# Ternary product in three bfloat16 parts, and one run for the keys and values of the latent attention

## The chip, the core and the metric

The kernel runs on one core of a Trainium2 chip. The metric is the device time of one execution in microseconds (us). TensorE is called PE here (its weight loads PEld), VectorE DVE, ScalarE ACT, GpSimd POOL, and SyncE SP; SP issues the transfers.

## The reference, cut to what matters

The input is 128 batches of 32 rows of 256 numbers (`x`) and 128 contexts of 257 rows of 256 (`ctx`). Six residual stages follow each other, each on rows normalised to mean 0 and variance 1. Stages 3 and 5 are the ones that the change touches:

```python
x = x + xattn0(ctx, layernorm(x))            # softmax attention of the rows on the context
x = x + selective_scan(layernorm(x))         # 512 channels, 16 states, a recurrence over 32 steps
x = x + ternary_ffn(layernorm(x))            # 256 -> 1024 -> 256
x = x + linear_attention(layernorm(x), ctx)
x = x + latent_attention(layernorm(x))       # 16 heads, latent of 64
x = x + quantised_ffn(layernorm(x))          # 8-bit rows, ternary weights

# ternary_ffn
h = layernorm(x) @ ternary(W_fc).T           # ternary: every weight is -1, 0 or 1
h = gelu(h); h = layernorm(h) * ln_w + ln_b
y = h @ ternary(W_proj).T

# latent_attention
lat = (x @ W_k + x @ W_v) @ W_down           # 64 numbers for a row
k = lat @ W_up_k; v = lat @ W_up_v; q = x @ W_q
s = (q . k) / 16 * exp(-0.01 * |i - j|); out = softmax(s) @ v; y = out @ W_o
```

## The kernel before, in words

The 4096 rows are 32 groups of 128 rows (four batches each), one row in each partition. `BLOCKS = (2, 4, 4, 4, 4, 4, 4, 4, 2)` puts the groups in nine blocks. For each group, `context_group` loads the context, forms keys and values (tiles `pkey`, `ku`, `pval`, `vf`, `pk`) and does the first attention. For each block, `scan_block` does the recurrence: four channel chunks of 16 states, and for every state an exponential on ACT (tile `a`), a scan on DVE (tile `h`) and a multiply-add on DVE (tile `acc`), 64 of each in a block; `pproj` holds the projections that go in, `pout` the product that comes out. Then `latent_group` runs four steps for each group: `mlp` (the ternary feed-forward), `linear`, `attention` (the latent attention) and `quantized_mlp`.

Nothing of this is issued in the order in which it is written. `Recorder.record` (L312) collects every operation with the engines that could do it and an assumed duration (`ns_of`, L42); `Recorder.order` (L378) then plays the whole program through in a list schedule: at each step it takes, among the operations that can start soon, the one that is due first. The due times come from the table `DUE` (L1445), one pair of start and end for each numbered part of the program (`begin`, L306, opens a part); `PRICE`, `WINDOW`, `SOONER`, `AHEAD` and `HORIZON` (L554) weigh the choice of an engine, how far a later start is allowed for an earlier due time, how early transfers are asked for, and how far ahead a tile may be opened. `R.either` is an operation for DVE or POOL, `R.copy` one for ACT or DVE. `together` (L276) joins a run of PE instructions into one step. `Recorder.trace` (L537) issues the result; L540 is the line that issues nearly everything, so the profile shows L540 for nearly all instructions and the tile names tell them apart. Each engine issues its list in that fixed order.

The PSUM tiles come from a ring of eight banks, the SBUF tiles from rings of 4 KB (`t4k`), 2 KB (`t2k`, 15 of them) and 1 KB (`t1k`, 7).

In `mlp` (L1171) the rows are transposed unnormalised and uncentred (`rows_T`, tile `xT`); the weights `w_fc` are float32 and have had the mean over the 256 inputs taken off in the set-up (`centred(w_fc, 2)`, L897), so that the product needs no centred rows. For each half of the 1024 outputs, two float32 matmuls fill a bank (tile `ph`):

```python
for k in range(2):
    ph = bank("ph")
    cols = slice(k * 512, (k + 1) * 512)
    with R.together():
        accumulate(ph, [(xT[:, dc, :], w_fc[:, dc, cols]) for dc in range(2)])
```

In `attention` (L1247) the queries (bank `pqa`, tile `qTa`), the latent (bank `plat`, tile `lat`), the keys (bank `pka`, tile `kd`), the scores (banks `psa`) and the softmax (tile `ea`) come one after the other; the values (bank `pva`, tile `vd`) are computed behind the softmax. ACT copies `qTa` ahead of `lat`.

Of the kernel before, what the change touches and what calls it, by code (L numbers as in the profile page):

```python
# [16 lines left out]
P = 128  # L17
# [74 lines left out]
    return 450  # L92


TAIL = {"vector": 75, "scalar": 100, "gpsimd": 25, "tensor": 130, "sync": 0}
HOP = {"vector": 38, "scalar": 38, "gpsimd": 80, "tensor": 55, "sync": 100}
TABLES = {AF.Exp: "exp", AF.Gelu: "gelu", AF.Sigmoid: "sigmoid"}
TABLE_NS = 1300
# [10 lines left out]
def size_of(a):  # L109
    n = 1  # L110
    for k in a.shape[1:]:
        n *= k
    return n
# [153 lines left out]
class Recorder:  # L267
# [8 lines left out]
    def together(self):  # L276

        recorder = self

        class Joined:  # L280
            def __enter__(self):
                recorder.joined = []

            def __exit__(self, *_):
                parts, recorder.joined = recorder.joined, None
                ways = {"tensor": ([c for p in parts for c in p[0]], sum(p[1] for p in parts), False)}
                recorder.add(ways, [r for p in parts for r in p[2]], [w for p in parts for w in p[3]])

        return Joined()

    def copy(self, out, in_):
        self.record({"scalar": ("copy", (out, in_), {}), "vector": ("tensor_copy", (out, in_), {})})

    def relu(self, out, in_):
        self.record({
# [10 lines left out]
    def begin(self, stage):  # L306

        self.stage = stage
        self.group += 1
        self.spans[self.group] = DUE[self.group]  # L310

    def record(self, calls):  # L312
# [31 lines left out]
        self.keep += bufs  # L344
        self.bufs_of.update((id(b), b) for b in bufs)
        if self.joined is not None:
            self.joined.append((*ways["tensor"][:2], reads, writes))
            return
        landing = 0
        if "sync" in ways:  # L350
# [200 lines left out]
                last[op.engine] = ins  # L551


PRICE = {"tensor": 0.0, "vector": 3.195, "scalar": 3.454, "gpsimd": 8.58, "sync": 0.0}  # L554
WINDOW = 31.919
SOONER = -0.015
AHEAD = 0
HORIZON = 0.832


@with_exitstack
def perceiver_kernel(ctx: ExitStack, tc: tile.TileContext, t: dict, out: bass.AP):
# [90 lines left out]
        return ring("t4", 4).tile(shape, name)  # L653

    def t2k(shape, name, dtype=F32):
        return ring("t2", 15).tile(shape, name, dtype)

    def t1k(shape, name, dtype=F32):
        return ring("t1", 7).tile(shape, name, dtype)
# [45 lines left out]
    R.begin("s")  # L705
    wqk = wts.tile([P, 2, D], F32, name="wqk")
    wkd = wts.tile([P, 2, LAT], F32, name="wkd")
    w_fc = wts.tile([P, 2, HID], F32, name="w_fc")
    w_pr = wts.tile([P, 8, D], F32, name="w_pr")
    s0 = wts.tile([P, D], F32, name="s0")  # L710
    w1 = wts.tile([P, 2, HID], BF16, name="w1")
# [132 lines left out]
    def late_setup():  # L844
# [49 lines left out]
                )  # L894

        ternary(w_fc, rows(t["w_fcT"]), [P, 2, HID], "fc", 1e-6, False)
        centred(w_fc, 2)  # L897
        ternary(w_pr, rows(t["w_prT"]), [P, 8, D], "pr", 1e-6, False)
        ternary(w1, rows(t["w1T"]), [P, 2, HID], "w1", 1e-5, True, g1)
        ternary(w2, rows(t["w2T"]), [P, 8, D], "w2", 1e-5, True, g2)  # L900
# [53 lines left out]
    def context_group(b0, xg, kvc):  # L954
# [83 lines left out]
            accumulate(py[:, 0:D], [(oT[:, dc, :], wv0[:, dc, :]) for dc in range(2)])  # L1038
        R.vector.scalar_tensor_tensor(xg, py[:, 0:D], rs, xg, ALU.mult, ALU.add)

        pk4 = bank("pk")
# [71 lines left out]
    def scan_block(x):  # L1115
# [15 lines left out]
        for ic in range(4):  # L1131
            pg = project(w_gate, ic * P)
            yg.append(t2k([P, TOK], "yg")[:, 0:tok])
            R.scalar.activation(yg[ic], pg, AF.Sigmoid, bias=b_gate[:, ic : ic + 1])
        for ic in range(4):

            dl = t2k([P, TOK], "dl")[:, 0:tok]
            R.scalar.activation(
                dl, project(w_in, DI + ic * P), AF.Relu, bias=b_in[:, 4 + ic : 5 + ic]
            )  # L1140
            xd = project(w_in, ic * P)
            acc = bank("acc")[:, 0:tok]
            R.scalar.activation(
                acc, xd, AF.Identity, bias=bd_in[:, ic : ic + 1], scale=d_vec[:, ic : ic + 1]
            )
            R.vector.scalar_tensor_tensor(xd, xd, b_in[:, ic : ic + 1], dl, ALU.add, ALU.mult)
            dv = dl.rearrange("p (b q) -> p b q", q=LQ)
            for s in range(NST):

                a = a_ring[s % NA][:, 0:batches, :]  # L1150
                R.scalar.activation(
                    a[:, :, 1:LQ], dv[:, :, 1:LQ], AF.Exp, scale=a_neg[:, ic, s : s + 1]
                )
                h = t2k([P, TOK], "h")[:, 0:tok]
                R.vector.tensor_tensor_scan(
                    h, a.rearrange("p b q -> p (b q)"), xd, 0.0, ALU.mult, ALU.add
                )
                R.vector.scalar_tensor_tensor(
                    acc, h, w_st[:, ic, s : s + 1], acc, ALU.mult, ALU.add
                )  # L1160
            R.vector.tensor_tensor(yg[ic], acc, yg[ic], ALU.mult)
        for g in range(size):
            po = bank("pout")
            with R.together():
                accumulate(
                    po[:, 0:D], [(yg[ic][:, g * P : (g + 1) * P], w_out[:, ic, :]) for ic in range(4)]
                )
            R.vector.tensor_tensor(x[g], po[:, 0:D], x[g], ALU.add)


    def mlp(xg):  # L1171

        _, r = stats(xg)
        xT = rows_T(xg)
        R.gpsimd.tensor_tensor(xg, xg, s0, ALU.add)
        hid = t4k([P, HID], "hid")
        st = tiny("st2", [P, 2, 6])
        for k in range(2):
            ph = bank("ph")
            cols = slice(k * 512, (k + 1) * 512)  # L1180
            with R.together():
                accumulate(ph, [(xT[:, dc, :], w_fc[:, dc, cols]) for dc in range(2)])
            R.scalar.activation(hid[:, cols], ph, AF.Gelu, scale=r)
            R.vector.bn_stats(st[:, k, :], hid[:, cols])
        mv = tiny("mv2", [P, 2])
# [61 lines left out]
    def attention(xg):  # L1247
# [3 lines left out]
        with R.together():  # L1251
            for c in range(2):
                accumulate(
                    pq[:, c * P : (c + 1) * P],
                    [(wqa[:, dc, c * P : (c + 1) * P], xT[:, dc, :]) for dc in range(2)],
                )
        qT = t1k([P, D], "qTa").rearrange("p (c n) -> p c n", c=2)
        R.scalar.copy(qT, pq[:, 0:D].rearrange("p (c n) -> p c n", c=2))

        pl_ = bank("plat")  # L1260
        with R.together():
            accumulate(pl_[0:LAT, 0:P], [(wkd[:, dc], xT[:, dc, :]) for dc in range(2)])
        lat = t1k([P, P], "lat")[0:LAT]
        R.scalar.copy(lat, pl_[0:LAT, 0:P])

        pk = bank("pka")
        with R.together():
            for c in range(2):
                accumulate(pk[:, c * P : (c + 1) * P], [(wupk[:, c * P : (c + 1) * P], lat)])
        kd = t2k([P, 2, GB, 2, LQ], "kd")  # L1270
        for r in range(2):
            R.scalar.activation(
                kd.rearrange("p c b r k -> p (c b) r k")[:, :, r, :],
                pk[:, 0 : 2 * P].rearrange("p (n q) -> p n q", q=LQ), AF.Copy,
                scale=odd[:, r : r + 1],
            )

        e = t2k([P, NH, LQ], "ea")
# [20 lines left out]
        R.vector.tensor_reduce(mx, e, AX.X, ALU.max)  # L1299
        R.gpsimd.tensor_tensor(e, e, mx.unsqueeze(2).to_broadcast([P, NH, LQ]), ALU.subtract)  # L1300
        R.scalar.activation(e, e, AF.Exp)

        vd = vds[turn[0] % NV]
        turn[0] += 1
        pv = bank("pva")
        with R.together():
            for b in range(GB):
                for r in range(4):
                    R.tensor.matmul(
                        pv[r * LQ : (r + 1) * LQ, b * 64 : (b + 1) * 64],  # L1310
                        lat[:, b * LQ : (b + 1) * LQ],
                        wupv.rearrange("p (j h k) -> p h j k", h=4, k=16)[:, r],
                        start=True, stop=True,
                    )
        for r in range(4):
            rows_ = slice(r * LQ, (r + 1) * LQ)
            R.scalar.copy(
                vd[rows_, :, :, r, 0:16],
                pv[rows_, 0 : GB * 64].rearrange("p (b j n) -> p b j n", b=GB, j=4),
            )  # L1320
        eT = t2k([P, 4, P], "eTa")
        transposed(e.rearrange("p h k -> p (h k)"), eT, 4)
        po = bank("poa")
# [84 lines left out]

    def latent_group(xg, kvc, rows_out):
        mlp(xg)  # L1410
        linear(xg, kvc)
        attention(xg)
        quantized_mlp(xg)
        R.sync.dma_start(rows_out, xg)

# [27 lines left out]


DUE = (  # L1445
    (-1.0, -0.9), (-0.011, 0.566), (-0.809, -0.789), (-0.212, 0.821), (-0.767, 0.109),
    (-0.01, 0.15), (0.299, 1.222), (0.556, 1.717), (1.591, 2.698), (1.87, 3.034), (0.619, 0.719),
    (0.863, 0.989), (1.148, 1.233), (1.17, 1.732), (1.498, 2.663), (2.591, 3.75425),
    (2.699, 3.86225), (2.806, 3.97), (2.915, 4.07825), (1.618, 1.802), (1.854, 2.163),
    (2.11, 2.23), (2.365, 2.485), (2.459, 3.663), (3.593, 4.75425), (3.7, 4.86225),  # L1450
    (3.807, 4.97025), (3.915, 5.07825), (2.571, 2.704), (2.985, 3.032), (3.115, 3.236),
    (3.365, 3.485), (3.5, 4.663), (4.591, 5.75425), (4.699, 5.86225), (4.807, 5.97025),
    (4.915, 6.07825), (3.61, 3.735), (3.864, 3.99), (4.115, 4.235), (4.365, 4.431), (4.5, 5.663),
    (5.591, 6.755), (5.699, 6.86225), (5.807, 6.97025), (5.915, 7.113), (4.615, 4.733),
    (4.866, 5.033), (5.115, 5.235), (5.365, 5.485), (5.5, 6.663), (6.612, 7.776), (6.72, 7.884),
    (6.7, 8.26), (6.921, 8.145), (5.616, 5.733), (5.924, 6.173), (6.117, 6.235), (6.462, 6.482),
    (6.501, 7.654), (7.288, 8.301), (7.441, 8.497), (7.544, 8.812), (7.594, 8.984),
    (6.632, 6.743), (6.921, 6.941), (7.171, 7.295), (7.361, 7.611), (7.495, 8.077),
    (7.815, 9.377), (7.667, 9.18), (7.008, 8.283), (7.34, 8.982), (7.658, 7.783), (7.829, 7.849),
    (8.0, 8.585), (8.023, 9.464), (8.392, 9.052),  # L1460
)


# [75 lines left out]
```

## Time and profile before

| | before |
|---|---|
| time, median of 3 runs | 1763.43 us (1761.84 to 1765.21) |
| profiled execution: its time, its span | 1760.93 us, 1759.2 us |
| PE busy | 1660.5 us (94%) in 17268 matmul instructions |
| DVE busy | 1554.4 us (88%) in 3083 instructions |
| ACT busy | 1430.8 us (81%) in 3442, with 114 table loads |
| POOL busy | 1117.0 us (63%) in 1827 |
| transfers | 59.69 MB, 34 GB/s |

The span runs from the first to the last instruction. A busy share is an average over the whole span; the stages differ, and what ends last in a stage sets its time. The clock that the profile lists beside a stage is the share of full speed that PE was granted. "Idle before" is time in which an engine's next instruction waited, with what it waited for.

### The profile page before, as it was taken

Reading aid. Unit: us, or ns where it says so; the run is one execution under the profiler, and the core shown is the slowest. Engines: PE = TensorE matmul, PEld = TensorE weight load, DVE = VectorE, ACT = ScalarE, POOL = GpSimd, SP = SyncE. Lnnn points to the kernel's source line nnn. Section 1 sums busy time; section 2 is a strip of 40 time slices with the busy share of each in tenths; the row PEclk is TensorE's granted clock in tenths of the full one; section 3 lists DMA queues with packets and bytes.
Section 4 is the critical chain, followed back from the end, with each engine's and each line's share of the span. In section 5 each row is a group of like instructions: output and inputs, shape, how many; then the busy total and the mean of one; then the engine's idle time right before and its main releaser. Section 6 shows DMA issues by size and latency. Waiting matters only on the chain.

```text
span 1759.2 us, 44923 instructions
## 1 busy us (share of the span) xinstructions
PE 1660.5 (94%) x17268; PEld 1211.7 (69%) x17299; DVE 1554.4 (88%) x3083; ACT 1430.8 (81%) x3442; POOL 1117.0 (63%) x1827
## 2 busy tenths in 40 slices
PE   8999999999999999999999999999999989597886
PEld 6787667766776777766776767766776667366564
DVE  3599799999898999899899999979999999999865
ACT  4587888888788997889788888889888898786655
POOL 5675556744776677666776747865776375347476
PEclk9999999999999999999999999999999999798886
DMA  7221101000110011001100021001100000000000
GB/s 243 74 83 47 61 29 32 29 31 4 48 42 2 16 59 35 29 2 40 41 29 29 7 65 37 29 2 40 40 29 29 1 8 20 4 4 5 5 4 22
DMA packets 44758, 59.69 MB, mean 34 GB/s; under 512 B 8704, under 2 KB 27008, under 8 KB 44544
## 3 DMA queue, kind: packets, MB, share of 16 engines
q1 hardware_dynamic: 44544, 56.81, 10.1%
q8 instruction: 137, 2.24, 0.5%
q14 instruction: 77, 0.63, 0.1%
HBM read 52.32 MB, written 4.19 MB: 32 GB/s over the span
## 4 chain that ended last, share of the span: by engine, by line
PE 75%; DVE 12%; ACT 7%; issue 1%; POOL 1%; DMA 0%; SPq 0%; DVEq 0%; ACTq 0%; POOLq 0%
PE pkey L540 13%; PE pval L540 11%; PE pproj L540 9%; PE pT L540 5%; PE pmlp L540 5%; DVE h L540 5%; PE ph L540 4%; PE pk L540 3%; PE pcT L540 3%; PE pout L540 3%; PE pq L540 3%; DVE acc L540 2%; PE psc L540 2%; PE pqa L540 2%; PE po L540 2%; PE pya L540 2%
## 5 line engine op out<-in xcount | busy, mean ns | idle before, releaser
L540 DVE TENSOR_TENSOR_SCAN h<-a,pproj 128x512 f32<-128x512 f32 (+1 forms) x576 | 617.4, 1087 | 12.4 <-ACT a L540 11.6
L540 ACT ACTIVATE a<-dl,a_neg 128x496 f32<-128x496 f32 (+1 forms) x576 | 369.8, 662 | 60.9 <-DVE h L540 57.6
L540 DVE SCALAR_TENSOR_TENSOR acc<-h,w_st,acc 128x512 f32<-128x512 f32 (+1 forms) x576 | 392.4, 681 | 0.1
L540 PE MATMUL pval<-wkv,cT 128*128 128x256 f32 x1024 | 245.7, 385 | 8.8 <-ACT hid L540 2.3
L540 PE MATMUL pkey<-wkv,cT 128*128 128x256 f32 x1024 | 238.1, 386 | 0.0
L540 POOL TENSOR_TENSOR ku<-ku,e 128x512 f32<-128x512 f32 x128 | 162.1, 1276 | 101.1 <-ACT ku L540 93.3
L540 PEld LDWEIGHTS pval<-wkv,cT 128*128 128x128 f32 x1024 | 189.6, 191 | 44.6 <-issue 7.4
L540 ACT ACTIVATE ks<-ku 128x256 f32<-128x256 f32 x512 | 208.1, 412 | 14.3 <-POOL ku L540 13.1
L540 PEld LDWEIGHTS pkey<-wkv,cT 128*128 128x128 f32 x1024 | 189.3, 190 | 37.7 <-issue 14.5
L540 POOL TENSOR_TENSOR ku<-ks,ku 128x512 f32<-128x512 f32 x128 | 163.7, 1285 | 29.8 <-ACT ks L540 29.1
L540 ACT ACT_TABLE_LOAD x114 | 146.3, 1283 | 5.1 <-PE ph L540 2.5
L540 POOL TENSOR_TENSOR kn<-kn,halves 128x4 f32<-128x4 f32 x128 | 134.1, 1048 | 22.5 <-ACT ks L540 21.7
L540 ACT ACTIVATE vf<-pval,kf 128x256 f32<-128x256 f32 x256 | 107.9, 471 | 40.0 <-PE pval L540 24.5
L540 POOL TENSOR_TENSOR rstd<-rstd,halves 128x1 f32<-128x1 f32 x224 | 123.7, 553 | 15.8
L540 POOL TENSOR_SCALAR rstd<-mv 128x1 f32<-128x1 f32 x224 | 42.9, 192 | 133.7 <-DVE mv L540 110.2
L540 PE MATMUL pproj<-xTs,w_in 128*128 128x512 f32 (+1 forms) x288 | 122.4, 552 | 0.5 <-ACT hT L540 0.2
L540 PE MATMUL ph<-w_fc,xT 128*128 128x512 f32 x256 | 120.2, 597 | 0.6 <-ACT xT L540 0.5
L540 PE MATMUL pmlp<-w_pr,hT 128*128 128x256 f32 x512 | 116.7, 381 | 1.5 <-ACT hT L540 1.2
L540 PEld LDWEIGHTS pmlp<-w_pr,hT 128*128 128x128 f32 x512 | 95.8, 190 | 20.7 <-issue 4.8
L540 ACT ACTIVATION_READ_ACCUMULATOR ks<-ku 128x1 f32 x512 | 99.4, 194 | 0.0
L540 ACT COPY cT<-pcT 128x512 f32<-128x512 f32 x128 | 71.8, 595 | 12.2 <-PE pcT L540 11.8
L540 DVE BATCH_NORM_STATS2 st<-x 128x6 f32<-128x256 f32 x192 | 78.7, 413 | 2.9 <-POOL x L540 1.7
(259 smaller groups left out, 3583.1 us busy)
## 6 DMA issues: line engine op xcount, KB each, us to landing
cx<-in_ctx_dram SPq DMA_DIRECT2D x64, 512.0 KB
x<-in_x_dram SPq DMA_DIRECT2D x32, 128.0 KB
cr<-in_ctx_dram SPq DMA_DIRECT2D x128, 32.0 KB
out_dram<-x SPq DMA_DIRECT2D x32, 128.0 KB
vlz<-vl SPq DMA_DIRECT2D x128, 1.1 KB
w_in<-in_w_inT_dram SPq DMA_DIRECT2D x1, 1024.0 KB
raw_fc<-in_w_fcT_dram SPq DMA_DIRECT2D x2, 512.0 KB
raw_pr<-in_w_prT_dram SPq DMA_DIRECT2D x2, 512.0 KB
```

The lines of the kernel that those rows point to most:

```text
L540: ins = getattr(engine, name)(*(traced(a) for a in args), **{k: traced(v) for k, v in kw.items()}).ins
```

## The change

In `mlp` the rows are now centred before they are transposed (`xc`). The transposed rows are then split into three bfloat16 parts (`x3`): the rounded value, the rounded remainder, and what is left. The ternary weights `w_fc` are kept in bfloat16, without the mean taken off, and each half of the product takes six bfloat16 matmuls in place of two float32 ones. In `attention` the latent is computed in the run and the bank of the queries and copied ahead of them, and the values are computed in the run and the bank of the keys. There are two more 2 KB tiles in the ring. The planner gets other constants, a `cast` that three engines can do, a surcharge for each joined run, more and smaller parts (`R.part()`, called within `context_group`, `scan_block` and `latent_group`), and a new table of due times with 251 pairs in place of 78.

```diff
-TAIL = {"vector": 75, "scalar": 100, "gpsimd": 25, "tensor": 130, "sync": 0}
+TAIL = {"vector": 75, "scalar": 90, "gpsimd": 25, "tensor": 215, "sync": 0}
...
-                ways = {"tensor": ([c for p in parts for c in p[0]], sum(p[1] for p in parts), False)}
+                small = any(p[4] for p in parts)
+                ns = sum(p[1] for p in parts) + (90 if small else 15)
+                ways = {"tensor": ([c for p in parts for c in p[0]], ns, False)}
...
+    def cast(self, out, in_):
+        self.record({
+            "scalar": ("copy", (out, in_), {}), "vector": ("tensor_copy", (out, in_), {}),
+            "gpsimd": ("tensor_copy", (out, in_), {}),
+        })
...
-PRICE = {"tensor": 0.0, "vector": 3.195, "scalar": 3.454, "gpsimd": 8.58, "sync": 0.0}
-WINDOW = 31.919
-SOONER = -0.015
-AHEAD = 0
-HORIZON = 0.832
+PRICE = {"tensor": 0.0, "vector": 0.379, "scalar": 0.104, "gpsimd": 0.438, "sync": 0.0}
+WINDOW = 45.022
+SOONER = 0.01
+AHEAD = 0.514
+HORIZON = 2.02
...
-        return ring("t2", 15).tile(shape, name, dtype)
+        return ring("t2", 17).tile(shape, name, dtype)
...
-    w_fc = wts.tile([P, 2, HID], F32, name="w_fc")
+    w_fc = wts.tile([P, 2, HID], BF16, name="w_fc")
...
-        centred(w_fc, 2)
...
     def mlp(xg):
-        _, r = stats(xg)
-        xT = rows_T(xg)
+        mv, r = stats(xg)
+        xc = t1k([P, D], "xc")
+        R.either.tensor_scalar(xc, xg, mv[:, 0:1], None, ALU.subtract)
+        xT = t1k([P, D], "xT")
+        transposed(xc, xT.rearrange("p (c n) -> p c n", c=2), 2)
+
+        x3 = t2k([P, 3, D], "x3", BF16)
+        R.cast(x3[:, 0, :], xT)
+        R.either.tensor_tensor(xT, xT, x3[:, 0, :], ALU.subtract)
+        R.cast(x3[:, 1, :], xT)
+        R.either.tensor_tensor(x3[:, 2, :], xT, x3[:, 1, :], ALU.subtract)
...
-                accumulate(ph, [(xT[:, dc, :], w_fc[:, dc, cols]) for dc in range(2)])
+                accumulate(ph, [
+                    (x3[:, k3, dc * P : (dc + 1) * P], w_fc[:, dc, cols])
+                    for dc in range(2) for k3 in range(3)
+                ])
...
     def attention(xg):
...
+            accumulate(pq[0:LAT, D : D + P], [(wkd[:, dc], xT[:, dc, :]) for dc in range(2)])
+        lat = t1k([P, P], "lat")[0:LAT]
+        R.scalar.copy(lat, pq[0:LAT, D : D + P])
...
-        pl_ = bank("plat")
-        with R.together():
-            accumulate(pl_[0:LAT, 0:P], [(wkd[:, dc], xT[:, dc, :]) for dc in range(2)])
-        lat = t1k([P, P], "lat")[0:LAT]
-        R.scalar.copy(lat, pl_[0:LAT, 0:P])
...
         pk = bank("pka")
+        pv = pk[:, D : 2 * D]
         with R.together():
             for c in range(2):
                 accumulate(pk[:, c * P : (c + 1) * P], [(wupk[:, c * P : (c + 1) * P], lat)])
+            for b in range(GB):
+                for r in range(4):
+                    R.tensor.matmul(
+                        pv[r * LQ : (r + 1) * LQ, b * 64 : (b + 1) * 64],
+                        lat[:, b * LQ : (b + 1) * LQ],
+                        wupv.rearrange("p (j h k) -> p h j k", h=4, k=16)[:, r],
+                        start=True, stop=True,
+                    )
...
+        for r in range(4):
+            rows_ = slice(r * LQ, (r + 1) * LQ)
+            R.scalar.copy(
+                vd[rows_, :, :, r, 0:16],
+                pv[rows_, 0 : GB * 64].rearrange("p (b j n) -> p b j n", b=GB, j=4),
+            )
...
-        pv = bank("pva")
-        with R.together():
-            for b in range(GB):
...
-DUE = ( ...
+DUE = ( ...
```

## The prediction

> **What bounds the kernel now.** First the busy shares and the slices: PE is at nine tenths nearly everywhere, and the fall comes only in the last sixth.
>
> ```profile
> PE 1660.5 (94%) x17268; PEld 1211.7 (69%) x17299; DVE 1554.4 (88%) x3083; ACT 1430.8 (81%) x3442; POOL 1117.0 (63%) x1827
> ...
> PE   8999999999999999999999999999999989597886
> ...
> DVE  3599799999898999899899999979999999999865
> ```
>
> Then the busy time by stretches, cut where the sum of a scan block (`pout`) is done: block 1 at 219 us, block 7 at 1398, block 8 at 1549, block 9 at 1665. Columns: stretch, length, busy time (and count) of PE, PEld, DVE, ACT, POOL, granted clock, DMA share, GB/s.
>
> ```profile
> 219.00:1398.00 1179.00, 1156.13 (x12221) 841.66 (x12242) 1088.73 (x2021) 1018.88 (x2438) 775.30 (x1259) 1.00 0.09 29
> 1398.00:1549.00 151.00, 123.45 (x1238) 89.91 (x1239) 147.37 (x268) 124.30 (x271) 76.61 (x134) 0.93 0.03 9
> 1549.00:1665.00 116.00, 99.89 (x1160) 71.19 (x1162) 104.96 (x283) 85.87 (x186) 63.35 (x105) 0.90 0.02 5
> 1665.00:1759.00 94.00, 73.13 (x714) 49.89 (x716) 57.64 (x166) 51.43 (x96) 67.42 (x120) 0.78 0.04 12
> ```
>
> Four regimes. To 1398 us PE is the bound: 98% busy, DVE 92%. From 1398 to 1549 DVE is: 147.4 of 151 us, PE 82%. From 1549 to 1665 DVE leads with 90%. The last 94 us are a tail behind the last scan, with no engine full. The chain of waits says the same: three quarters of it is PE.
>
> ```profile
> PE 75%; DVE 12%; ACT 7%; issue 1%; POOL 1%; DMA 0%; SPq 0%; DVEq 0%; ACTq 0%; POOLq 0%
> ```
>
> Transfers (0%) bound nothing, so the loads' new order on SP is costed at nothing; the cover is a DMA share of 0.09, and a late one would show as a DMA wait.
>
> **PE's part.** The timeline of PE shows spacings. Four `ph` records are two float32 matmuls of 512 columns (two passes each); `phq` is a bfloat16 product of the same width that the kernel already has:
>
> ```profile
> 1554.33 1.88 PE L540 MATMUL ph<-w_fc,xT 128*128 128x512 f32 x4
> 1556.05 3.62 PE L540 MATMUL pmlp<-w_pr,hT 128*128 128x256 f32 x16
> ```
> ```profile
> 1685.53 1.03 PE L540 MATMUL phq<-w,qT 128*128 128x512 bf16 x4
> 1686.40 0.38 PE L540 MATMUL pT<-ident,x 128*128 128x128 f32 x2
> ```
>
> From start to start, half a product takes 1.72 us now; a bfloat16 matmul of the same width takes 0.87 / 4 = 0.217 us, so six take 1.30. Saved: 0.42 us a half, 64 halves, 26.9 us. The set-up loses `centred(w_fc)`, four float32 matmuls of 0.86 us: 3.4. The latent, the values and the keys are the same matmuls in other runs: 0. PE's sum is -30.3 us.
>
> The Trainium skill's page "TensorE: Matmul & The Clock Gate", section on the back-to-back issue gap, gives about 131 ns sustained for 512 columns; six would then take 0.79 us and the saving would be 60 us. No row here runs at that rate, and the 217 ns of the row is used.
>
> **What the parts cost elsewhere.** The listing of the built program tells which engine got each new step. Per kind, with the nearest rows:
> - DVE gets 16 of the 32 centrings (0.35 us: between 0.286 for a one-operand `e<-isp` and 0.439 for `xn`), 8 casts (0.29), 38 subtractions (0.415, as `oa`), two more `ku` (0.685): 25.1 us. It loses the mean's removal, 2 x 0.69 + 2 x 1.27 = 3.9. Sum +21 us; durations overlap (on DVE busy time is 0.88 of their sum), so +19 busy.
> - POOL gets 16 centrings and 14 casts (0.40, as `q<-xn`) and 26 subtractions (0.73, as `x<-x,s`): +31 us. Its 37% idle hides them.
> - ACT gets 42 casts (0.37, as `xT`: +15.5) and loses 6 of 114 table loads (1.283 each: -7.7) and two `ku` (-1.2): +6.6, hidden beside 14% idle in the PE-bound stretch.
>
> The chain from the transposed rows to `ph` gets two casts and two subtractions longer, 1.6 to 2.3 us with hops of about 0.1, and everything behind `ph` in PE's fixed list would wait. In the listing, PE's work between the transposition and the first `ph` is 2.7 to 22 us, median 8.5 (before: 0 to 16, median 2.4). The needed cover is a copy (0.37) and that chain, some 2.5 us, so nothing; without cover it is 32 x 2.5 = 80 us. Likewise the earlier `lat` and `vd` copies: ACT does `lat` ahead of `qTa`, the kd copies wait for 16 more small matmuls (0.6 us), under a PE list with 2 to 3 us between the runs.
>
> **The sum, stretch by stretch,** pricing both listings up to the same markers:
> 1. To the end of block 7: PE's list is 1366 us long before and 1349 after. The saving on 22 groups and the set-up (22) is partly filled by other work (one more quantised feed-forward and one attention, less one `mlp`). PE stays the bound: DVE would be at 94% here. -17.
> 2. Block 8: the new list has less latent work here, DVE's priced sum is 147 in place of 168 (x0.875). 147 us of busy time become 129, plus 3.6 idle: -18.
> 3. Block 9: 140.6 in place of 124.5, 104.8 busy become 118 plus 11 idle: +13.5.
> 4. Tail: ten quantised feed-forwards in place of eight are left, five attentions in place of six; DVE's priced sum is 78 in place of 63, POOL gets some 12 us on 67. Between 0 (packed into idle time) and +22 (stretched with DVE's work, 57.6 to 71). The tail's chain alternates between DVE, POOL and PE, with engines at 55 to 78%, so I take +9, nearer to the low end.
>
> Together -12.5 us: span 1746.7. The profiled execution took 1760.9, 1.7 over its span, and the median of the runs is 2.5 above that, 4.2 above the span. 1763.4 - 12.5 gives 1751; I say 1750.
>
> **Rivals.**
> *The shared port (ends slower).* Every new DVE step reads two SBUF tiles or is a plain copy or scalar step. The trace shows what such a step does beside POOL:
>
> ```profile
> 338.12 1.44 DVE L540 TENSOR_SCALAR xn<-x,mv,rstd 128x256 f32<-128x256 f32 x1
> 338.13 1.27 POOL L540 TENSOR_TENSOR ku<-ku,e 128x512 f32<-128x512 f32 x1
> 339.47 1.27 POOL L540 TENSOR_TENSOR ku<-ks,ku 128x512 f32<-128x512 f32 x1
> ```
>
> It lasted 1.44 us, until POOL's step was over; its median is 0.405. So 62 steps could wait up to 1.03 us each, 64 us of DVE. In the PE-bound stretch (two thirds: 43 us) DVE's 1089 us and its own 13 of new work would come to 1145, level with PE's 1139 (1156 less 17), and I count 10 of the 17 us gained there as lost; in blocks 8, 9 and the tail 20 steps add up to 21 us directly. At that price 1750 + 21 + 10 = 1781. It decides from a mean wait of 0.65 us, at which 13 us of the gain are gone. Against: `xn` has a mean of 0.439, so its mean wait is 0.03 to 0.1 us, and its wait on POOL is a matter of where the planner puts it.
>
> The Trainium skill's page "SBUF — State Buffer", section "SBUF: two separate sides", speaks against the change: DVE's second port pair is POOL's, and whoever holds it blocks the other for the whole instruction. By that rule a wait is what is left of POOL's step, about 0.6 us at a POOL share of 0.65, 0.4 us in the mean, and the sum would be 8 us less gain; the row agrees that it happens, and `xn`'s mean says seldom.
>
> *The tail packs (faster still).* If the extra backlog fits the tail's idle time (+0) and block 9's 11 us of DVE idle time are filled by it, the sum is -33 and the time 1730.
>
> *The gain is lost in the order (no change).* If PE in the long stretch idles 3% in place of 2% (the six-part products wait for banks or rows now and then), 12 us go and it stays at 1763.
>
> That the change doesn't do what it says is excluded: the listing has 384 bfloat16 `ph` matmuls and no float32 one.
>
> **How the numbers follow.** The sum above, 1737 to 1759: 0.48. Tail packs, 1718 to 1737: 0.24. No change, 1759 to 1768: 0.11. Port, or a tail at its full price on top of one: 1768 to 1790: 0.17. A range of 1722 to 1774 leaves out some 0.05 below and 0.12 above. A measurement here tells 0.2% (3.5 us) from no change; faster by more than that takes the first two cases, 0.72; within it 0.09; slower 0.19.
>
> **What would show it.** Right: `ph` in 384 bfloat16 records at about 217 ns, block 7's last `pout` near 1381 us, PE still at 98% before it, 151 us of block 8 down to about 132, block 9 up to about 130, a tail of about 103. Wrong: DVE above 97% in the long stretch with new steps far above 0.42 us (port); PE waiting for ACT's, DVE's or POOL's parts `x` ahead of `ph` (cover too short); a tail over 115.

## The result, and the profile after

The changed kernel is slower: 1779.91 us (median of 4 runs, 1775.81 to 1780.45) beside 1762.63 us (1759.63 to 1765.21) for the kernel before, a ratio of 1.0094 [1.0071, 1.0116]. The profiled execution took 1780.3 us, its span is 1778.3.

First the page after: busy time by engine, the slices of PE and DVE, and the chain of waits.

```profile
PE 1657.9 (93%) x17366; PEld 1215.5 (68%) x17419; DVE 1576.7 (89%) x3143; ACT 1433.7 (81%) x3476; POOL 1156.7 (65%) x1883
...
PE   7899999998999999999999999999999967888886
...
DVE  4579699988998999999999998998999999997966
...
PE 59%; DVE 19%; ACT 12%; POOL 5%; issue 3%; DMA 1%; POOLq 0%; SPq 0%; DVEq 0%; ACTq 0%
```

PE has 30 us of matmuls less and is busy 2.6 us less. Its share of the chain fell from 75% to 59%; DVE, ACT and POOL took that up. Then the stretches, cut at the same markers (the last `x<-pout` of block 1, 7, 8 and 9); columns as before.

```profile
217.00:1400.00 1183.00, 1153.36 (x12427) 843.59 (x12466) 1111.98 (x2072) 1034.68 (x2502) 805.54 (x1290) 0.99 0.10 31
1400.00:1538.00 138.00, 109.95 (x760) 77.83 (x763) 130.01 (x213) 103.50 (x209) 67.22 (x119) 0.88 0.01 5
1538.00:1673.00 135.00, 115.63 (x1403) 85.29 (x1405) 117.92 (x331) 87.64 (x216) 76.44 (x130) 0.84 0.01 2
1673.00:1778.00 105.00, 79.40 (x868) 54.70 (x873) 71.18 (x195) 64.98 (x118) 79.41 (x137) 0.83 0.04 14
```

| | before | predicted | after |
|---|---|---|---|
| end of block 7 | 1398.5 | 1381 | 1400.0 |
| block 8 | 150.7 | 132 | 138.2 |
| block 9 | 115.9 | 130 | 134.9 |
| tail | 93.8 | 103 | 104.9 |

The later stretches moved the way that was forecast, but in sum to +17.6 us in place of +4.5. The long one, where 17 us were to be gained, gained nothing: PE is 97.5% busy there as before (98%), with 22 groups' products shortened.

The products themselves did get shorter. In PE's timeline a whole product of six matmuls lasts 1.46 us; one matmul alone lasts 0.39 in the mean, so five spacings take 1.07, or 0.215 us each, as priced.

```profile
417.45 1.46 PE L553 MATMUL ph<-w_fc,x 128*128 128x512 bf16 x6
```

So the gain was used up elsewhere on PE. Groups of PE instructions over the whole execution; the columns behind the count are busy us, mean ns of one, then the idle time of PE just before them with what ended it. Before:

```profile
L540 PE MATMUL ph<-w_fc,xT 128*128 128x512 f32 x256 | 120.2, 597 | 0.6 <-ACT xT L540 0.5 <-DVE hq L540 0.2
L540 PE MATMUL pT<-ident,hid 128*128 128x128 f32 x256 | 38.5, 277 | 1.3 <-ACT hid L540 1.3
L540 PE MATMUL poq<-w,qT 128*128 128x256 bf16 x256 | 36.6, 291 | 5.5 <-ACT qT L540 5.4
```

After:

```profile
L553 PE MATMUL ph<-w_fc,x 128*128 128x512 bf16 x353 | 90.7, 387 | 9.9 <-DVE h L553 4.6 <-POOL x L553 1.6 <-DVE p L553 1.1
L553 PE MATMUL pT<-ident,hid 128*128 128x128 f32 x256 | 41.2, 295 | 11.4 <-ACT hid L553 7.1 <-DVE h L553 3.4 <-DVE x L553 0.6
L553 PE MATMUL poq<-w,qT 128*128 128x256 bf16 x256 | 36.9, 293 | 7.2 <-ACT qT L553 5.8 <-DVE h L553 1.3
L553 PE MATMUL pT<-ident,xc 128*128 128x128 f32 x64 | 12.5, 286 | 5.5 <-POOL xc L553 3.1 <-ACT hid L553 1.9 <-ACT pTl L553 0.5
```

`ph` and the transposition of `hid`, which hardly waited, now wait 20 us more; but only 5 of these 20 lie in the long stretch (2.7 and 3.5 us there, beside 0.2 and 1.1 before), the rest behind it. All of PE's idle time in the long stretch, its length less PE's busy time, grew from 22.9 us to 29.6. The rest doesn't show as idle time: a record of `ph` lasts 0.387 us in the mean while the next starts 0.215 us after it, so a wait shorter than the difference counts as busy. Adding up, over the long stretch, how much later each matmul starts than an undisturbed run of its kind would let it gives 198.5 us before and 226.0 after (worked out from the records of PE). Of the 27.5 us between, some 5 are no waits: 24 of the 264 records of `ph` there are missing from the trace. The 22 that are left are more than the 18.5 us that 22 groups' products save there (22 x 2 x 0.42): the saving went into many small delays. Some 6.5 us of them are clock: in three spells of the long stretch, 13.7 us together, PE was granted half its clock, so that `ph` at 428 us starts a matmul every 0.427 us in place of 0.216. Before has no such spell there. Each stands behind a wait of PE of 1.9 to 3.4 us; whether the wait brings it on was not tested, and in e14 (below) a wait of 3.1 us had none behind it.

### The profile page after: what moved, and what is told of

Read it like the earlier page. It is cut to its first block, busy times and chain, and to the rows that moved or that the text cites. A ratio compares the mean times of both kernels' runs of the same rounds, so it can differ in the third digit from the quotient of the medians.

```text
span 1778.3 us, 45250 instructions
## 1 busy us (share of the span) xinstructions
PE 1657.9 (93%) x17366; PEld 1215.5 (68%) x17419; DVE 1576.7 (89%) x3143; ACT 1433.7 (81%) x3476; POOL 1156.7 (65%) x1883
## 4 chain that ended last, share of the span: by engine, by line
PE 59%; DVE 19%; ACT 12%; POOL 5%; issue 3%; DMA 1%; POOLq 0%; SPq 0%; DVEq 0%; ACTq 0%
PE pval L553 9%; PE pkey L553 9%; DVE h L553 8%; PE pproj L553 7%; PE pT L553 5%; PE pmlp L553 4%; DVE acc L553 4%; PE pqa L553 3%; PE pk L553 3%; PE pq L553 2%; POOL ku L553 2%; PE pka L553 2%; PE pcT L553 2%; PE pout L553 2%; ACT a L553 2%
## 5 line engine op out<-in xcount | busy, mean ns | idle before, releaser
L553 PE MATMUL pval<-wkv,cT 128*128 128x256 f32 x1024 | 249.8, 392 | 13.3 <-ACT ku L553 4.2
L553 PEld LDWEIGHTS pmlp<-w_pr,hT 128*128 128x128 f32 x512 | 98.1, 195 | 17.6 <-ACT hT L553 2.1
L553 PE MATMUL ph<-w_fc,x 128*128 128x512 bf16 x353 | 90.7, 387 | 9.9 <-DVE h L553 4.6
L553 PEld LDWEIGHTS pproj<-xTs,w_in 128*128 128x128 f32 x288 | 51.1, 192 | 37.8 <-issue 30.5
```

What stands on the lines that cost most here:

```text
L553: ins = getattr(engine, name)(*(traced(a) for a in args), **{k: traced(v) for k, v in kw.items()}).ins
```

## The experiments

Theories: (1) the split's own steps and their chain eat the gain; (2) the new order does; (3) the merged runs of the attention do; (4) PE was not alone the bound. Runs on different chips differ by some 2 us, so runs are compared by their ratio to the kernel before on the same chip; "us" behind a ratio is (ratio - 1) x 1763. On this scale the change is +16.6. The intervals are some 4 us wide on each side.

### The parts, with the order planned anew

e1 is the changed kernel with `mlp` of before, e2 with `attention` of before, e3 with both (only the planner's part of the change is left), e4 the kernel before with the changed `attention`. e1 and e3 also have the float32 centred weights and the 15 tiles of 2 KB of before.

```diff
 # e1 (e3 too)
-                accumulate(ph, [
-                    (x3[:, k3, dc * P : (dc + 1) * P], w_fc[:, dc, cols])
-                    for dc in range(2) for k3 in range(3)
-                ])
+                accumulate(ph, [(xT[:, dc, :], w_fc[:, dc, cols]) for dc in range(2)])
 # e2 (e3 too); e4 the other way round
-            accumulate(pq[0:LAT, D : D + P], [(wkd[:, dc], xT[:, dc, :]) for dc in range(2)])
+        pl_ = bank("plat")
```

> The changed kernel with the float32 ternary product and the centred float32 weights put back; attention and planner stay changed. Theory 1, the three-part split costs more on DVE, POOL and ACT (62 + 56 + 42 short steps) than PE's 30 us bring: the time falls back to about 1763 us or below. Theory 2, the planner's new constants and due times feed PE late, and the split is worth its PE time: PE gets 30 us more to do, and the time rises to 1795 us or more. Theory 3, the merged attention runs cost it: no fall, 1775 to 1800 us.

> The changed kernel with the attention of before. Theory 3 (merged runs hold the keys back behind 16 more small matmuls and let the latent wait in the run of the queries): down by 10 us or more, to 1770 us or below. Theories 1 and 2: within 8 us of the changed kernel's 1780, either way, as any edit shifts the order.

> Only the planner of the change (constants, surcharges, parts, due times); product and attention as before. Theory 2: slower than before by 20 us or more, 1783 us up. Theory 1: at 1763 us, or faster. Theory 3: as theory 1.

> Only the merged attention runs, with the planner and the product of before. Theory 3: slower than before by 10 us or more, 1773 us up. Theories 1 and 2: 1763 us within 6, a little faster if the freed banks help.

Measured: e1 1925.86 us (1.0906 [1.0885, 1.0927]), e2 1836.58 (1.0406 [1.0386, 1.0427]), e3 1942.05 (1.0983 [1.0951, 1.1014]), e4 1799.45 (1.0205 [1.0159, 1.0251]). All are slower than both kernels, by up to 180 us, which is more than the work of any part; e4 issues the same matmuls as before. The likely reason, not tested by itself, is that a table of due times fits one list of operations, and that with another list the planner puts everything elsewhere. So these four say nothing on theories 1 to 3. e4 lies where theory 3 had put it, but it can't tell the merged runs from the new placing, and theory 3 stays untested. From here on the order is kept: the planner places the operations of the one kernel, and only what is issued at a place is changed.

### What the shorter product is worth in the order of before

e5: the order of before, each product as six bfloat16 matmuls of rounded rows; no centring, no split, no mean taken off the weights.

```diff
-        xT = rows_T(xg)
+        xT = t1k([P, 2, P], "xT", BF16)
+        transposed(xg, xT, 2)
...
-                accumulate(ph, [(xT[:, dc, :], w_fc[:, dc, cols]) for dc in range(2)])
+                accumulate(ph, [
+                    (xT[:, dc, :], w_fc[:, dc, cols]) for dc in range(2) for _ in range(3)
+                ])
```

> Before's order of every engine kept to the instruction; only the ternary product is issued as six bfloat16 matmuls (all six on the rounded rows, so the value is three times that of rounded rows: no split steps, no centring, no mean taken off the weights). PE gets 30 us less to do and no engine more. Theory 1, PE was the bound to 1398 us and the split's own steps ate the gain later: 1763 less 17 to 27, 1736 to 1746 us. Theory 4, PE at 98% was already fed just in time by DVE, ACT and POOL and so not alone the bound: less than 8 us faster, 1755 us up. Theory 2, the order of the change loses it: as theory 1.

Measured: 1744.36 us, 0.9895 [0.9871, 0.992], -18.5 us. Block 7 ends at 1378.2. Its long stretch:

```profile
214.00:1378.00 1164.00, 1135.81 (x12296) 834.14 (x12342) 1087.22 (x2021) 1017.68 (x2438) 777.26 (x1259) 1.00 0.09 29
```

PE is busy for 20 us less, and the stretch is 15 us shorter. Of 30 us of PE work, 61% come off the time: in the order of before it is mostly PE that sets the pace, and the size of the saving was right.

### The order of the change, with work left out

Each keeps the order of the changed kernel. e6 doesn't issue the second cast and the two subtractions (all six matmuls read the first part); e7 leaves out the four matmuls of the second and third part; e9 leaves out `acc` of two of 16 states; e10 is e7 and e9 together; e17 leaves out one of the two halves of every sum in `pval`; e18 that and `acc` of four states. The lines below stand for what is not issued; the planner still places the whole list.

```diff
 # e6
-        R.either.tensor_tensor(xT, xT, x3[:, 0, :], ALU.subtract)
-        R.cast(x3[:, 1, :], xT)
-        R.either.tensor_tensor(x3[:, 2, :], xT, x3[:, 1, :], ALU.subtract)
 # e7, e10
-                    for dc in range(2) for k3 in range(3)
+                    for dc in range(2) for k3 in range(1)
 # e9, e10 (e18: s % 4 == 2)
+                R.left_out = s in (5, 11)
                 R.vector.scalar_tensor_tensor(
                     acc, h, w_st[:, ic, s : s + 1], acc, ALU.mult, ALU.add
 # e17, e18
-                    [(cT[:, dc, j * P : (j + 1) * P], wkv[:, 1, dc, :]) for dc in range(2)],
+                    [(cT[:, dc, j * P : (j + 1) * P], wkv[:, 1, dc, :]) for dc in range(1)],
```

> The changed kernel's order kept; the second cast and both subtractions are not issued, and all six bfloat16 matmuls read the first, rounded part (the value is three times that of rounded rows). PE's list is unchanged; DVE loses some 20 us, ACT some 8, POOL some 20. Theory 1: 15 us or more faster than the changed kernel, 1765 us or below. Theory 2: within 6 us of it, 1774 to 1780. Theory 4: in between, 1765 to 1774.

> The changed kernel's order kept, with the whole split; only the two matmuls of the first part are issued in each half of the ternary product, four of six left out (the value is that of the rounded rows). PE loses 256 x 0.216 = 55 us. If PE is still the bound of the changed kernel to 1400 us: 30 us or more faster, 1750 us or below. Theories 1 and 4, other engines end last there now: less than 15 us faster, 1765 us up. Theory 2 says nothing sharp, 1750 to 1765.

> The changed kernel's order kept to the instruction, but the multiply-adds (acc) of two of the 16 states are not issued: 72 steps of 0.68 us, 49 us less of DVE, the counterpart of the 55 us of PE that the one-part product left out (which gained 3.5 us). If DVE has become the bound of this order: 35 to 49 us less than the changed kernel, 1731 to 1745. If PE and DVE hold each other (PE's list waits for DVE at some places, DVE's for PE at others): 10 to 30 less, 1750 to 1770. If neither list binds and the time lies in waits on ACT and POOL: within 5 of 1780.

> The changed kernel's order, with both left out: two of the six bfloat16 matmuls of a product stay (55 us less of PE), and the multiply-adds of two of 16 states (49 us less of DVE). If DVE alone binds: no more than the run with the multiply-adds alone, plus 3.5. If PE and DVE cover each other: the sum is more than the parts by 10 us or more, 1710 to 1740. If ACT and POOL bind: within 8 of 1780.

> The changed kernel's order, PE relieved everywhere and not only in the product: of the values' product in every context group (pval) one of the two halves of the sum is left out, 512 records, about 110 us of PE's 1658. If PE and DVE are full side by side in the new order, so that each alone keeps the pace: 2 to 12 us less than the changed kernel. If PE is after all the bound, but at other places than the product: 50 or more.

> The same, and the multiply-adds (acc) of four of the 16 states are left out as well: 144 steps of 0.68 us, 98 us of DVE. Two of 16 alone gave 3 us. If PE and DVE are full side by side: clearly more than both parts together, 18 to 40 us less than the changed kernel (with 208 us of work gone). If ACT, POOL or waits that no engine's load sets keep the pace: no more than 15.

| | left out | time, ratio | against the change |
|---|---|---|---|
| e6 | split: DVE 17, POOL 22, ACT 5 (busy) | 1773.58, 1.006 [1.0044, 1.0075] | -6.0 us |
| e7 | PE 55 us, in the product | 1776.36, 1.0076 [1.0061, 1.0091] | -3.2 |
| e9 | DVE 49 us | 1776.79, 1.006 [1.0038, 1.0082] | -6.0 |
| e10 | both | 1774.18, 1.0038 [1.0022, 1.0054] | -9.9 |
| e17 | PE 110 us, in all groups | 1759.24, 0.9963 [0.9943, 0.9983] | -23.1 |
| e18 | that and DVE 98 us | 1751.93, 0.9909 [0.988, 0.9938] | -32.6 |

The long stretch of e7, and of e10:

```profile
216.00:1399.00 1183.00, 1125.37 (x12246) 826.70 (x12278) 1111.20 (x2069) 1033.93 (x2502) 806.91 (x1290) 0.99 0.10 31
```
```profile
219.00:1394.00 1175.00, 1125.05 (x12288) 825.06 (x12277) 1083.09 (x2021) 1032.87 (x2502) 805.01 (x1290) 0.99 0.10 31
```

e6 lies on the border of what theories 2 and 4 had expected, and 9 us short of what theory 1 had. In e7 PE is busy 28 us less and the stretch lasts 1183 us, as with all six matmuls. So PE at the product does not set the pace of this order, although it is 95% busy; nor does DVE (e9, which lies between two of its forms). e10 is no more than the sum of e7 and e9: PE and DVE do not cover each other there, since that form asked for 10 us above the sum. Between DVE alone (up to 9.5 us by these figures) and waits on ACT and POOL (up to 8) its 9.9 doesn't decide. A microsecond of PE work at the product is worth 0.06, spread over all groups 0.21, in the order of before 0.61. Theory 4 as it was put (PE fed just in time) fits e7. Against waits alone speaks e17: PE's work all over the span is worth something. But the sharper form that e17 and e18 were to test, PE and DVE full side by side, isn't shown: e17 gave more than that form allowed, and e18 no more than its parts (23 and twice 6). The chain of waits of e18 passes through four engines:

```profile
PE 48%; ACT 17%; DVE 15%; POOL 15%; issue 4%; DMA 0%; POOLq 0%; SPq 0%; ACTq 0%; DVEq 0%
```

What is left as the bound of this order is that passing from list to list. That is argued from the runs in which neither PE nor DVE alone brought much, not shown, and which of the waits lead in it stays open.

### The change's own steps in the order of before

e14 is e5 with the centring (on DVE, between the statistics and the transposition). e11 has the centring and the split (ACT, DVE, ACT, DVE), that is, the whole product of the change, with the attention, the constants and the due times of before. e12 has two parts and four matmuls. e13 is the kernel before without `acc` of two states. Their new steps are put into the lists where their inputs are ready, with tiles of their own; the first rounding is done straight from the bank, without the change's plain copy.

```diff
 # e14, e11, e12
+        xc = own("xci", 3).tile([P, D], "xc")
+            ("vector", ("tensor_scalar", (xc, xg, mv[:, 0:1], None, ALU.subtract), {}), 330),
 # e11
+            ("vector", ("tensor_tensor", (xc, pt[:, 0:D], x3[:, 0], ALU.subtract), {}), 440),
+            ("scalar", ("copy", (x3[:, 1], xc), {}), 400),
+            ("vector", ("tensor_tensor", (lo, xc, x3[:, 1], ALU.subtract), {}), 390),
 # e12, e15
+            ("vector", ("tensor_tensor", (x3[:, 1], pt[:, 0:D], x3[:, 0], ALU.subtract), {}), 440),
```

> The kernel before, its order kept, six bfloat16 matmuls of rounded rows, and of the change's other steps only the centring (32 steps on DVE between the statistics and the transposition); the two casts and subtractions of the split are left out. Without the centring the same matmuls gave 1744, with centring and split 1776. If the centring holds PE up, because PE's list has the transposition right behind the rows: 1758 to 1768. If the split's chain behind the transposition does: 1745 to 1753.

> The kernel before, its order of every instruction kept, with the change's product alone put in between: rows centred on DVE, transposed, split into three bfloat16 parts (ACT, DVE, ACT, DVE), six bfloat16 matmuls, weights not centred. Attention, planner constants and due times are those of before. The six matmuls without the split gave 1744 in this order. If the split's own steps and their chain eat the gain (theory 1): 1763 or more; DVE gets 38 us more (32 x 1.2) in an order with DVE at 92%, and PE waits for a chain of 2 us up to 32 times. If the gain is lost in the new order (theory 2): 1745 to 1757.

> As the run before, but the rows are split into two bfloat16 parts (the rounded value and the rounded remainder, 16 bits of the 24), four matmuls for half a product: 28 us less of PE than with three, one cast and one subtraction less in the chain. If the chain and DVE's steps decide: 15 to 35 us below the run with three parts. If PE does: 10 to 20 below it, 1728 to 1745. This could be faster than both kernels.

> The kernel before, its order kept, the multiply-adds (acc) of two of 16 states not issued: 49 us less of DVE, as in the run on the changed kernel's order (which gained 3 us). If before's order is bound by PE to the end of block 7 and by DVE only in block 8: 3 to 10 us less, nearly all in blocks 8 and 9, where 16 of the 72 steps lie. If PE and DVE were both tight in it: 15 or more.

Measured: e14 1756.09 us (0.9971 [0.9952, 0.999], -5.1), e11 1775.65 (1.0059 [1.0043, 1.0075], +10.4), e12 1763.5 (0.999 [0.9973, 1.0007], -1.8: 12 below e11, as expected if PE decides, but no faster than before), e13 1758.58 (0.9969 [0.9952, 0.9987], -5.5). From e5 on, the centring costs 13.4 us and the split 15.5: together 29, more than the 18.5 gained, as theory 1 had it for this order; e14 came out between the two values expected, since both steps cost about the same. DVE's work is worth 0.11 of itself in this order, so it is not the 43 us of e11's new DVE steps that count but who waits for them. e13's gain has the size that was expected, but not the place: it was to lie in blocks 8 and 9, and these last as long as before in its profile (151.2 and 116.0 us, beside 150.7 and 115.9), though DVE is busy for 3.5 and 2.4 us less. So DVE, busy for 147 of 151 us in block 8, does not set the pace there by its load, as far as one profile tells. The transpositions in `mlp`, in e5 (where they read `x`, with those of other steps) and in e14:

```profile
L544 PE MATMUL pT<-ident,x 128*128 128x128 f32 x192 | 36.9, 280 | 2.9 <-DVE x L544 1.9 <-DVE y L544 0.9
```
```profile
L602 PE MATMUL pT<-ident,xc 128*128 128x128 f32 x64 | 12.9, 284 | 16.7 <-DVE xc L602 16.4 <-DVE x L602 0.3
```

PE stands still for 16.7 us ahead of 32 transpositions, half a microsecond each: statistics, centring and hop lie where nothing lay.

The centring can be avoided. e15 reads uncentred rows: rounded rows and remainder by the weights (four matmuls), and the rounded rows by minus the mean of the weights over the inputs (two more, from a bfloat16 tile). It keeps 16 of the rows' 24 bits and takes the mean from the rounded rows alone.

```diff
+                ("matmul", (ph, part[:, dc * P : (dc + 1) * P], w), ...)
+                for k3, part in enumerate((hi, hi, lo)) for dc in range(2)
+                for w in (w_mean[:, cols] if k3 == 1 else w_fc[:, dc, cols],)
```

> The kernel before, its order kept, the rows not centred: a product is the rounded rows and the remainder by the ternary weights (four bfloat16 matmuls) and the rounded rows by minus the mean of the weights over the inputs (two more), so no step lies between the rows and the transposition; DVE gets one subtraction a group more (32 x 0.44 = 14 us), whose result the last two matmuls of six need. If the centring's wait is what cost 15 to 25 us in this order: 1745 to 1756, faster than both kernels. If the subtraction behind the transposition is what costs: 1757 to 1765.

Measured: 1748.11 us, 0.9917 [0.9891, 0.9943], -14.6 us: faster than both kernels. Of the 18.5 us only some 4 are lost, no more than the intervals can tell, though there is one subtraction more in each group; `ph` waits 3.5 us, beside 2.9 in e5. Its long stretch:

```profile
214.00:1383.00 1169.00, 1139.95 (x12301) 836.24 (x12346) 1095.64 (x2048) 1017.30 (x2439) 775.34 (x1259) 1.00 0.09 29
```

### POOL's centring

In the changed kernel POOL has half of the centrings, and they take 0.94 us where the prediction had 0.40 and the planner assumes 0.48. The groups of both engines:

```profile
L553 POOL TENSOR_SCALAR xc<-x,mv 128x256 f32<-128x256 f32 x16 | 15.1, 942 | 0.2
...
L553 DVE TENSOR_SCALAR xc<-x,mv 128x256 f32<-128x256 f32 x16 | 6.2, 392 | 0.0
```

e8 writes the step with a second operation (times 1.0), in the hope that the form set its length; e16 issues POOL's 16 on DVE at the same places.

```diff
 # e8
-        R.either.tensor_scalar(xc, xg, mv[:, 0:1], None, ALU.subtract)
+        R.either.tensor_scalar(xc, xg, mv[:, 0:1], 1.0, ALU.subtract, ALU.mult)
 # e16
+            if op.engine == "gpsimd" and any(b.name == "xc" for b in op.bufs):
+                op.engine = "vector"
```

> The changed kernel, same order, with the centring given as subtract and multiply by one: on POOL the subtraction alone took 0.94 us where two-operation steps of the same size took 0.40. If the form sets that time, the 16 centrings on POOL fall to 0.40 to 0.50 us and the transpositions behind them wait less: 3 to 8 us faster than the changed kernel, 1772 to 1777 us. If the pointer operand sets it, no change: 1780 us within 3.

> The changed kernel's order, the 16 centrings that POOL has (0.93 us each where the planner assumed 0.48) issued on DVE at the same places (0.39). If POOL's long step delays the lists behind it: 4 to 8 us less than the changed kernel, 1772 to 1776. If its time lies beside other work, as the prediction had it, or DVE has no room for it: 1778 to 1782.

e8 gave 1778.52 us (1.0088 [1.0071, 1.0105]) and missed its aim: POOL's step became longer, 1.147 us in the mean, with no effect on the time. e16 gave 1776.69 (1.0079 [1.005, 1.0107]), 2.7 us less than the change by the ratios; that is within what the intervals can tell, so at most a small part lies there.

## Why the prediction was wrong, step by step

**Step 1, to the end of block 7, is the one that failed: "PE stays the bound: DVE would be at 94% here. -17".** DVE is at 94.0%, and the stretch ends 1.5 us later, not 17 earlier. The product was priced rightly (0.215 us a matmul; e5 gained 18.5), but I took what PE work is worth from the order of before and carried it over to another order. e7 shows that in the new one it is worth a tenth of that (of the next 55 us of PE work 3.2 came off the time). PE's 98% could not show this: the new order has 97.5%, and the saving does not come off its long stretch. Of the prediction's signs only the end of block 7 (1400 us, not 1381) told it: PE at 98% was to be a sign of being right, and none of the three signs of being wrong came up clearly (DVE is at 94%, the tail at 105 us, and in the long stretch `ph` waited 0.5 us for POOL's `x`).

**The cover.** I let the split be hidden by PE's list between transposition and `ph`, "so nothing". In the new order it costs 6.0 us (e6), so nearly right, while in the order of before it costs 15.5. But the chain was begun at the transposed rows. The centring lies ahead of them, and I priced only the engine time of its 32 steps, not the wait of the transposition; in the order of before that is 13.4 us (e14), in the new one PE's idle time ahead of `pT<-ident,xc` is 5.5 us.

**The order.** e6 and e14 do the same `mlp` work in the two orders, but for one plain cast a group and half of the centrings on POOL in e6: 1.006 and 0.9971. The new order, with the merged attention in it, is 15.7 us slower at this work, though it hides the split better. Adding up: matmuls -18.5, centring +13.4, split +15.5 make +10.4 (e11) in the order of before; the new order's +6.2 is what is left to the +16.6 measured, and it contains the better hiding of the split. So the product's own steps, put into the order of before with nothing else changed, cost more than its matmuls save. Merged attention and due times could not be parted.

Why the new order falls short is argued, not shown. Replaying both issue orders with the planner's new constants gives 1746 us for the order of before and 1735 for the new one, a gain of 11. The chip follows the first within 6 us at the end of every block and is 13 us late at the end; behind the second it is late by 12 us at block 7, 18 at block 8, 33 at block 9 and 43 at the end. With the durations of the traces in place of the assumed ones both replays get longer, the new order's by more; by how much depends on how overlapping durations are counted. That fits a plan with less slack, met by steps that are longer than planned. The one such step that was tested, POOL's `xc` (e16), makes 2.7 us of it, within what the intervals can tell, so the cause of the new order's part stays open.

**Steps 2 to 4** had the right sign and the busy times (DVE 130.0 and 117.9 in blocks 8 and 9, forecast 129 and 118). Too small was DVE's idle time: 8 in place of 3.6 us, and 17 in place of 11. That DVE bounds block 8 is not borne out: with less of its work there the block lasted as long (e13). So the forecast of 132 us, which was built on it, may have come near the measured 138 partly by luck. The tail came to 104.9, forecast 103.

**The engines.** DVE +22 (forecast +19), POOL +40 (+31; its centrings alone make 9 of the difference), ACT +3 (+7), table loads 108 as listed.

**The rivals.** The shared port gave nearly the right time, 1781, for a reason that isn't there: it needed a mean wait of 1.03 us for that time and of 0.65 to lose the gain, and DVE's first subtraction, the worst of the new steps, lasts 0.558 in the mean and 0.418 in the median, 0.14 us longer for each of 18.

```profile
L553 DVE TENSOR_TENSOR xT<-xT,x 128x256 f32<-128x256 f32 x18 | 10.0, 558 | 0.9 <-ACT x L553 0.6 <-POOL x L553 0.3
```

The estimate that the prediction worked out from the Trainium skill's page "SBUF — State Buffer", section "SBUF: two separate sides", was 0.4 us a step; no run here shows such a wait to weigh in the sum. "The gain is lost in the order" had the mechanism, with banks and rows that come late: PE's visible idle share in the long stretch went from 1.9% to 2.5%, where it had 2% to 3%. But it was given 0.11 and stopped at no change.

## What to carry to other kernels

An engine's busy share does not say what its work is worth: shorten the work in the order as it stands, without the new steps, and see how much of it comes off the time. Where a schedule is planned anew, that price holds for the old order only. And a step that is put ahead of a producer costs its latency at every place where the consumer stood right behind it, so the chain is counted from the first new step, not from the one where the data path begins.

## What was not expected of the hardware

- A subtraction of a per-row scalar from 128x256 takes POOL 0.94 us and DVE 0.39; with a multiplication by 1.0 added, POOL takes 1.147. A POOL step of the same size without that scalar, but with a bfloat16 result (`q<-xn`), takes 0.41 (0.40 before).
- Taking 104 us of work off two engines at 94% and 97% changed the time by 10 us of 1780 (e10).
